# The end of layer 0 written out: the last two rows of a two-layer attention kernel in an order of their own

## The chip, the cores and the metric

The kernel runs on one core of a Trainium2 chip. The metric is the device time of one execution in microseconds (us). Five engines run their own instruction streams and meet at semaphores: TensorE (PE; its weight loads are shown apart as PEld), VectorE (DVE), ScalarE (ACT), GpSimd (POOL) and SyncE (SP), which here issues DMAs.

## The reference

The input x has 128 rows of 256 positions and 256 channels. Two layers follow each other, each of the form "x plus attention of the group-normalised x":

```python
# layer 0: 8 heads of 32 channels; one attention of 256 x 256 in each of the 128 rows
x = x + _L0_conv_ref(_gn(x), pair_repr, gate_proj, qkv_proj, out_proj, bias_proj)
# layer 1: 4 heads of 64 channels, keys at most 16 positions away
x = x + _L1_conv_ref(_gn(x), w_in, b_in, w_out, b_out, 16)
```

In layer 0 a row's attention is

```python
bias = einsum('nijz,zh->nhij', pair_repr, bias_proj)     # the same for all rows
gate = sigmoid(x @ gate_proj)
sim  = softmax(q @ k.T * scale) + bias                   # the bias is added after the softmax
out  = ((sim @ v) * gate) @ out_proj
```

The normalisation `_gn` takes mean and variance over all rows and positions of a group of 8 channels. Layer 1 can therefore not start before the last row of layer 0 has been added up and counted.

## The kernel before

**Layer 0, the steady part.** Rows are numbered s = 0 to 127 (S = 128) and go in pairs. The loop `for s in range(S)` works on row s, finishes row s - 1 and, in the same turn, projects the next pair: q and k in an even turn, values and gate in an odd one (`stretch`). Each projection, each output projection and each bias product of a pair is done with seven block products in place of eight (a Strassen-like scheme: `Seven`, `Output`, `biased`), which needs sums of blocks made beforehand: `sum_values` and `out_sums` on GpSimd, `sum_bias` once on VectorE. One of the four blocks of the bias is overwritten by such a sum; its original is kept in DRAM as `bias_far`, for a fallback that runs only where a softmax sum is out of range.

In a turn, a row passes through these steps:

- `scores(s, half)`, L838 and L851: the products k times q of four heads into four PSUM banks (`sim`), and their exponentials on ScalarE into `ex`, 128x512 each.
- `join_tiles`, L860: VectorE adds the two key tiles of the exponentials (`both`), two heads in one instruction.
- `sum_heads`, L883: TensorE sums `both` over the keys for all eight heads (`zs`).
- `divide`, L963 to L969: VectorE takes the reciprocal `rz`; SP writes it to DRAM (`rz0_far`) and reads it back four times, broadcast over the partitions (`near`). For the last row only, `spread_last` (L981, L982) does this with two TensorE products and a copy.
- `totals` and `least`, L989 and L996: the sum and the minimum of `zs`, for the fallback's condition.
- `attend`, L870: the exponentials times v (`av`, a PSUM bank).
- `biased`, L934 to L956: the bias times v for a pair of rows, seven products in one PSUM bank (`pbv`); after most of them ScalarE or VectorE takes a part out (`bv`).
- `weighted` (L1011) and `gated` (L1023, L1024): av times near, plus bv, times the gate, into `at`.
- `output`, L590 with L701 to L723: the output projection of a pair in seven products (`po`); VectorE takes every one out and adds the row itself (`xt`), into `o`.
- `settle`, L1058: VectorE counts the pair into `stats1` (mean and variance by parts), and SP stores it to DRAM (`x1`).

**Layer 0, the end.** The last turns (s = 126 and 127) are in the same loop with conditions (`s < S - 2`, `s >= S - 2`): no pair is left to project. What remains of the bias products of rows 126-127 and the seven-product output of rows 124-125 runs in them. After the loop, row 127 is finished, and rows 126 and 127 get their output by `one_by_one`: sixteen products, and one addition by VectorE (`finish`, L1050).

**Statistics.** `Most` joins the parts in `stats1` ahead of the end: two shares, one in turn 125 and one in turn 126 (L291 to L295), into a tile `most`. At the end `channel_columns` copies that tile and the three last parts into one tile `last` (L301, L302), joins them (L308), copies the means (L310), and takes the mean and variance over the groups with two small TensorE products (L313, L322). `keep_on` puts products with no use between them (`warm`, L1173).

**Order.** TensorE, ScalarE, VectorE and SP run in the order of the program text in this part (`manual_schedule`); GpSimd's order is the scheduler's. Eight PSUM banks hold all: a ring of five for projections, scores, outputs and `near`, and one each for `zs`, `pbv` and `av`. A product that wants a bank of the ring waits until the one five places earlier has been read out.

**Layer 1** begins with the loads of its first rows (`load1`, L794), VectorE's normalisation (L1237) and the products `p1v` (L1274).

Of the kernel before, what the change touches and what calls it, by code (L numbers as in the profile page):

```python
# [9 lines left out]
F32 = mybir.dt.float32  # L10
# [5 lines left out]
P = 128  # L16
# [23 lines left out]
def conv_preact_kernel(  # L40
# [59 lines left out]
    def strip(a):  # L100
        return slice(B * a, B * (a + 1))
# [173 lines left out]
    class Most:  # L275


        def __init__(self, pool, stats, late, which):
            self.stats, self.late = stats, late
            n = stats.shape[2] - late  # L280
            self.shares = ((0, n // 2), (n // 2, n))
            self.mv = pool.tile([P, 2, 2, 2], F32, name=f"mv_most{which}")

            self.most = pool.tile([P, 2, 2, 3], F32, name=f"most{which}")

        def join(self, share):
            n0, n1 = self.shares[share]
            count = (n1 - n0) * 2.0 * R
            nc.gpsimd.memset(self.most[:, :, share, 0:1], count)
            for half in range(2):  # L290
                nc.vector.bn_aggr(  # L291
                    out=self.mv[:, half, share, :], in_=self.stats[:, half, n0:n1].rearrange("p n s -> p (n s)")
                )
            nc.vector.tensor_copy(self.most[:, :, share, 1:2], self.mv[:, :, share, 0:1])
            nc.vector.tensor_scalar(self.most[:, :, share, 2:3], self.mv[:, :, share, 1:2], count, None, op0=ALU.mult)  # L295

    def channel_columns(pool, most, which, wait=lambda n: None):

        stats, late = most.stats, most.late
        last = pool.tile([P, 2, 2 + 2 * late, 3], F32, name=f"last{which}")  # L300
        nc.vector.tensor_copy(last[:, :, 0:2], most.most)  # L301
        nc.vector.tensor_copy(  # L302
            last[:, :, 2:].rearrange("p h e k -> p h (e k)"),
            stats[:, :, stats.shape[2] - late :].rearrange("p h n s -> p h (n s)"),
        )
        mv = pool.tile([P, 2, 2], F32, name=f"mv{which}")
        for half in range(2):
            nc.vector.bn_aggr(out=mv[:, half, :], in_=last[:, half].rearrange("p e k -> p (e k)"))  # L308
        means = pool.tile([P, 2], F32, name=f"means{which}")
        nc.vector.tensor_copy(means, mv[:, :, 0])  # L310
        wait(5)
# [463 lines left out]
    with ExitStack() as both:  # L775
        st1 = both.enter_context(tc.tile_pool(name="st1", bufs=1))

        stats1 = st1.tile([P, 2, S // 2 + 1, 6], F32, name="stats1")
        quarters1 = {w: Quarters(st1, w_in_t, n * C, f"1{w}") for n, w in enumerate("qk")}
# [17 lines left out]
        with ExitStack() as lay0:  # L797
# [57 lines left out]

            def join_tiles(s, half, j):

                if s < S:
                    ex, both = hd[s, half]
                    nc.vector.tensor_tensor(both[:, j : j + 2], ex[:, j : j + 2, 0, :], ex[:, j : j + 2, 1, :], ALU.add)  # L860

            def products(to, s, weights):

                i, r = divmod(s, 2)
                v = res["v", i]
                for half in range(2):
                    for kt in range(2):
                        for j in range(4):
                            c0 = kt * P + j * D0
                            nc.tensor.matmul(  # L870
                                to[D0 * j : D0 * (j + 1), half, :],
                                lhsT=v[:, 2 * r + half, c0 : c0 + D0], rhs=weights(4 * half + j, kt),
                                start=(kt == 0), stop=(kt == 1),
                            )
# [84 lines left out]
            def divide(s, zs):  # L959
                if s < 0:  # L960
                    return
                rz = att.tile([P, R], F32, tag="rz", name=f"rz{s}", bufs=1)
                nc.vector.reciprocal(rz, zs[:, 0, :])  # L963
                near = att.tile([P, 2, R], F32, tag="near", name=f"near{s}", bufs=1)
                if s < S - 1:
                    far = rz0_far[s % 2]
                    nc.sync.dma_start(out=far.rearrange("j h q -> (j h) q"), in_=rz[0 : P : B // 2])
                    for j in range(A):
                        nc.sync.dma_start(  # L969
                            out=near[strip(j)].rearrange("p h q -> p (h q)"),  # L970
                            in_=far[j].rearrange("h q -> (h q)").partition_broadcast(B),
                        )
                hd[s, "rz"] = rz
                hd[s, "zs"], hd[s, "near"] = zs, near

            def spread_last(s):

                rz, near = hd[s, "rz"], hd[s, "near"]
                ps = proj_bank(f"near{s}")
                for half in range(2):  # L980
                    nc.tensor.matmul(ps[:, half, :], lhsT=spread0[:, half], rhs=rz, start=True, stop=True)  # L981
                nc.scalar.copy(near, ps)  # L982

# [69 lines left out]
            def settle(s, first, k, part):  # L1053
# [3 lines left out]
                for half in range(2):  # L1057
                    nc.vector.bn_stats(out=stats1[:, half, part, :], in_=o[:, first : k + 1, half, :])  # L1058
                if k == XG - 1:
# [20 lines left out]
            with tc.manual_schedule(  # L1080
# [11 lines left out]
                nc.sync.dma_start(out=bias_far, in_=bias_blocks[0, 1])  # L1092
                most1 = Most(st1, stats1, 3, 1)
                for s in range(S):
                    exps = scores(s, 0)
# [20 lines left out]
                    if s % 2 == 0:  # L1116
                        settle_pair((s - 4) // 2)
                    if S - 3 <= s < S - 1:
                        most1.join(s - S + 3)
                    normal(s + 4)  # L1120
                    third, fourth = scores(s, 1)
                    if s % 2 == 1 or s >= S - 2:
                        third()
# [8 lines left out]
                    total = lambda: totals(s - 1)  # L1132
                    rests = iter((third, fourth, total) if s % 2 == 0 and s < S - 2 else (fourth, total))

# [5 lines left out]
                    if s % 2 == 1 and s > 1:  # L1140
                        out_sums((s - 3) // 2)
                        po, work = output((s - 3) // 2, work), ()
                    if s < S - 2:
                        stretch(
                            ("qk", "vg")[s % 2], s // 2 + 1, (EARLY, PLAIN)[s % 2], rest, bias, po,
                            work if s % 2 == 0 else (),
                        )
                        work = work if s % 2 == 1 else ()
                    else:
                        rest()  # L1150
                        for _ in range(2 if s % 2 == 0 else 3):
                            next(bias)
                            next(po, None)
                            next(po, None)
                        for _ in po:
                            pass
                        if s % 2 == 0:
                            next(bias)
                    if s >= S - 2:
                        rest()  # L1160
                    for job in work:
                        job()
                    if s % 2 == 1 and s < S - 2:
                        sum_rows((s + 3) // 2)
                        sum_values(s // 2 + 1)
                load1(0)
                load1(1)
                warm = proj_bank("warm")

# [4 lines left out]

                gated(S - 2)
                outputs.pop(S // 2 - 2).take(4)
                least(S - 2)
                divide(S - 1, sum_heads(S - 1))
                totals(S - 1)
                attend(S - 1)  # L1180
                spread_last(S - 1)
                weighted(S - 1)
                gated(S - 1)
                settle_pair(S // 2 - 2)
                for s in (S - 2, S - 1):
                    if s == S - 1:
                        keep_on(4)
                    for _ in one_by_one(out_sb, st[s]["at"], f"po{s}", lambda ps: st[s].update(po=ps), B):
                        pass
                    finish(s)  # L1190
                mean1, rstd1 = channel_columns(st1, most1, 1, keep_on)
# [379 lines left out]
    with tc.If(sure < P):  # L1571
        with ExitStack() as lay:
# [10 lines left out]
            )  # L1583
            nc.sync.dma_start(out=bias_sb[:, 0, :, P : 2 * P], in_=bias_far)
            stats2 = one.tile([P, 2, S // 2, 6], F32, name="stats2")

# [127 lines left out]
            for g in range(S // XG):  # L1714
                x3 = two.tile([P, XG, 2, R], F32, tag="x3", name=f"x3_{g}")
                nc.sync.dma_start(out=x3, in_=rows(x1, g * XG, XG))
                for k in range(0, XG, 2):
                    for half in range(2):
                        nc.vector.bn_stats(
                            out=stats2[:, half, (g * XG + k) // 2, :], in_=x3[:, k : k + 2, half, :]  # L1720
                        )
            most2 = Most(one, stats2, 1, 2)
            for share in range(2):
# [29 lines left out]
```

## Time and profile before

| | |
|---|---|
| time, median of 3 runs (lowest to highest) | 3100.07 us (3099.98 to 3102.68) |
| the profiled execution: time, span of the core | 3099.65 us, 3098.0 us |
| busy: TensorE, its weight loads | 3009.3 us (97%), 2058.7 us (66%) |
| busy: VectorE, ScalarE, GpSimd | 2259.0 us (73%), 1911.1 us (62%), 1903.9 us (61%) |
| mean granted TensorE clock | 0.992 |
| first score product of row 126 | 1987.67 us |
| first product of layer 1 (p1v) | 2028.60 us |

The span is the time from the first to the last instruction of the core; the execution's time has 1.65 us more. In the lines of the profile "L838" is line 838 of the kernel; a tile's name stands without its number; "out<-in" names what is written and read; "x32" counts instructions as the chip executes them, and one matrix product of 32-bit numbers is two of them. In a timeline the first number is the start in us from the span's start and the second the duration. In the chain of waits a line is a piece of the path that ended last. The granted clock is 1.00 at full speed.

### The profile page before, as it was taken

Reading aid. Unit: us, or ns where it says so; the run is one execution under the profiler, and the core shown is the slowest. Engines: PE = TensorE matmul, PEld = TensorE weight load, DVE = VectorE, ACT = ScalarE, POOL = GpSimd, SP = SyncE. Lnnn points to the kernel's source line nnn. Section 1 sums busy time; section 2 is a strip of 40 time slices with the busy share of each in tenths; the row PEclk is TensorE's granted clock in tenths of the full one; section 3 lists DMA queues with packets and bytes.
Section 4 is the critical chain, followed back from the end, with each engine's and each line's share of the span. In section 5 each row is a group of like instructions: output and inputs, shape, how many; then the busy total and the mean of one; then the engine's idle time right before and its main releaser. Section 6 shows DMA issues by size and latency. Waiting matters only on the chain.

```text
span 3098.0 us, 142607 instructions
## 1 busy us (share of the span) xinstructions
PE 3009.3 (97%) x62733; PEld 2058.7 (66%) x62733; DVE 2259.0 (73%) x4523; ACT 1911.1 (62%) x4321; POOL 1903.9 (61%) x1916
## 2 busy tenths in 40 slices
PE   7779999999999999999999999999999999999997
PEld 4546666666666666666666666567777777777775
DVE  4667787778877887788778877746666666666665
ACT  4656666666666666666666666645555555555553
POOL 3035666666656565656565656457777777767774
PEclk9989999999999999999999999999999999999999
DMA  9942222222222222222222222114444444444443
GB/s 381 424 130 50 56 65 62 57 55 65 61 58 55 65 62 58 55 65 62 60 53 65 62 59 54 58 58 103 98 98 105 98 104 93 103 100 103 99 97 71
DMA packets 384789, 280.86 MB, mean 91 GB/s; under 512 B 285232, under 2 KB 353312, under 8 KB 378016
## 3 DMA queue, kind: packets, MB, share of 16 engines
q1 hardware_dynamic: 383264, 269.29, 32.9%
q8 instruction: 494, 8.09, 1.1%
q0 software_dynamic: 752, 2.36, 0.2%
q14 instruction: 135, 1.11, 0.1%
q10 hardware_dynamic: 144, 0.00, 0.0%
HBM read 202.38 MB, written 69.18 MB: 88 GB/s over the span
## 4 chain that ended last, share of the span: by engine, by line
PE 91%; DMA 5%; DVE 2%; POOL 1%; ACT 0%; issue 0%; SPq 0%; DVEq 0%; POOLq 0%; ACTq 0%
PE sim L838 9%; PE p1v L1274 7%; PE av L870 7%; PE p1q L590 7%; PE pbv L934 6%; PE po L590 6%; PE p1k L590 6%; PE p1o L590 6%; PE pq L590 6%; PE pv L590 6%; PE pk L590 5%; PE pg L590 5%; PE zs L883 4%; PE 1sim L1295 3%; DMA pr<-in_L_conv_pair_repr_dram 3%; PE 1av L1336 3%
## 5 line engine op out<-in xcount | busy, mean ns | idle before, releaser
L851 ACT ACTIVATE ex<-sim 128x512 f32<-128x512 f32 x1024 | 554.8, 605 | 256.6 <-PE sim L838 256.6
L860 DVE TENSOR_TENSOR both<-ex 128x512 f32<-128x512 f32 x512 | 449.5, 897 | 67.0 <-ACT ex L851 66.8
L634 POOL TENSOR_TENSOR v<-v,midv 128x512 f32<-128x512 f32 x64 | 82.1, 1283 | 453.8 <-ACT v L628 453.8
L838 PE MATMUL sim<-q,k 32*64 32x256 f32 x8192 | 289.6, 389 | 1.3 <-ACT ex L851 1.3
L963 DVE RECIPROCAL rz<-zs 128x256 f32<-128x256 f32 x128 | 225.0, 1758 | 67.2 <-PE zs L883 51.9
L870 PE MATMUL av<-ex,v 128*32 128x256 f32 x4096 | 244.5, 379 | 1.6 <-DVE at L1024 1.6
L694 ACT ACTIVATE 1q<-p1q,bqk 128x256 f32<-128x256 f32 x192 | 91.1, 475 | 240.7 <-PE p1q L590 129.7
L1305 POOL TENSOR_TENSOR 1p<-1ex,seen 128x768 f32<-128x768 f32 x127 | 231.6, 1824 | 12.4 <-ACT 1ex L1303 12.4
L1274 PE MATMUL p1v<-w_in_t,1xn 128*64 128x128 f32 x4096 | 236.2, 273 | 0.1
L1274 PEld LDWEIGHTS p1v<-w_in_t,1xn 128*64 128x64 f32 x4096 | 231.4, 137 | 6.1 <-issue 0.5
L838 PEld LDWEIGHTS sim<-q,k 32*64 32x64 f32 x8192 | 152.2, 131 | 113.3 <-issue 66.4
L582 POOL TENSOR_TENSOR 1ts<-1xn 128x512 f32<-128x512 f32 x64 | 81.4, 1272 | 232.0 <-ACT 1xn L1235 232.0
L634 POOL TENSOR_TENSOR q<-q,midq 128x512 f32<-128x512 f32 x64 | 82.0, 1282 | 196.1 <-ACT q L628 196.1
L870 PEld LDWEIGHTS av<-ex,v 128*32 128x32 f32 x4096 | 131.5, 110 | 79.2 <-DVE at L1024 2.1
L1405 DVE TENSOR_TENSOR 1at<-1av,1near 128x512 f32<-128x512 f32 x128 | 82.6, 686 | 132.7 <-DMA 1near<-rz_far 103.6
L1312 POOL TENSOR_TENSOR 1zp<-1p 128x512 f32<-128x512 f32 x127 | 162.4, 1278 | 10.0
L1281 ACT COPY 1v<-p1v 128x512 f32<-128x512 f32 x128 | 75.1, 586 | 125.0 <-PE p1v L1274 125.0
L346 DVE BATCH_NORM_STATS2 stats<-xs 128x6 f32<-128x128 f32 x512 | 100.3, 277 | 63.7 <-DMA xs<-in_x_dram 63.7
L883 PE MATMUL zs<-both,place 128*32 128x256 f32 x2048 | 139.2, 389 | 0.5 <-DVE both L860 0.5
L1023 DVE TENSOR_TENSOR av<-av,bv 128x512 f32<-128x512 f32 x128 | 89.5, 700 | 62.8 <-ACT bv L956 60.5
L1373 DVE RECIPROCAL 1rz<-1z 128x64 f32<-128x64 f32 (+1 forms) x192 | 129.8, 678 | 2.2
L688 DVE SCALAR_TENSOR_TENSOR 1o<-p1o,bo_v,yg 128x256 f32<-128x256 f32 x183 | 88.6, 484 | 56.1 <-PE p1o L590 53.2
(340 smaller groups left out, 8348.9 us busy)
## 6 DMA issues: line engine op xcount, KB each, us to landing
pr<-in_L_conv_pair_repr_dram SPq DMA_DIRECT2D x32, 1024.0 KB
xs<-in_x_dram SPq DMA_DIRECT2D x16, 2048.0 KB
x<-o SPq DMA_DIRECT2D x64, 512.0 KB
yg<-x SPq DMA_DIRECT2D x64, 512.0 KB
out_dram<-1o SPq DMA_DIRECT2D x256, 128.0 KB
near<-rz_far SPq DMA_DIRECT2D x508, 64.0 KB
xg<-in_x_dram SPq DMA_DIRECT2D x252, 128.0 KB
1near<-rz_far SPq DMA_DIRECT2D x124, 256.0 KB
```

Source lines behind the costliest of these rows:

```text
L590: nc.tensor.matmul(out[cols], lhsT=lhsT[:, cols], rhs=rhs, **flags)
L634: nc.gpsimd.tensor_tensor(self.to[:, 2:4], self.to[:, 2:4], self.mid, ALU.add)
L838: nc.tensor.matmul(sims[j][KB * c : KB * (c + 1), kt, :], lhsT=k[p0 : p0 + D0, 2 * r + half, k0 : k0 + KB], rhs=q[p0 : p0 + D0, 2 * r + ha ...
L851: nc.scalar.activation(ex[:, j], sims[j], AF.Exp, scale=1.0 / math.sqrt(D0))
L860: nc.vector.tensor_tensor(both[:, j : j + 2], ex[:, j : j + 2, 0, :], ex[:, j : j + 2, 1, :], ALU.add)
L870: nc.tensor.matmul(to[D0 * j : D0 * (j + 1), half, :], lhsT=v[:, 2 * r + half, c0 : c0 + D0], rhs=weights(4 * half + j, kt), start=(kt == ...
L883: nc.tensor.matmul(zs[strip(j), 0, :], lhsT=place0[:, half, :], rhs=both[:, j, :], start=(half == 0), stop=(half == 1),)
L934: nc.tensor.matmul(ps[strip(j), acc, half, :], lhsT=stationary[n][:, half, strip(j)], rhs=bias_of[n][:, 4 * half + j, :], start=(n <= 2 an ...
L963: nc.vector.reciprocal(rz, zs[:, 0, :])
L1274: nc.tensor.matmul(ps[KB * half : KB * (half + 1), b, :], lhsT=xns[i][:, 2 * r + kt, KB * b : KB * (b + 1)], rhs=w_in_t[:, kt, 2 * C + P * ...
L1305: engine.tensor_tensor(p.rearrange("p j (r c) -> p (j r) c", c=WROW)[:, :, 0 : 2 * WSTEP] .rearrange("p r (t c) -> p r t c", c=WSTEP)[:, : ...
L1312: engine.tensor_tensor(zp, p[:, :, 0:R], p[:, :, R : 2 * R], ALU.add)
```

## The change

The loop ends at row 125, and the rest is written out.

- The first-half scores of a row, its second-half scores and the other row's products are put in one order by hand. Row 126's and 127's scores are issued earlier among the other products.
- The bias products of rows 126 and 127 are plain products by row (`bias_row`: sixteen products by `products`, then one copy) in place of the seven products of the pair. For this the first bias block is read back from `bias_far` into its place after row 125, by SP, ahead of layer 1's first two loads.
- The outputs of rows 124 and 125 are plain too (`plain_output`); ScalarE copies them to a tile `o_last` and GpSimd adds the rows (`residual`).
- The reciprocals of rows 125 and 126 are spread by TensorE (`spread_row`), not through DRAM, as for row 127 before. `keep_av` copies `av` to the SBUF tile, and the product `near` stays in PSUM: the reverse of before.
- GpSimd makes one of the two joins of key tiles (`join_tiles`) of row 126's second half and row 127's first half. For row 127's second half there is none: TensorE sums the exponentials themselves over both key tiles.
- The two joins of statistics come one turn sooner (turns 124 and 125), with four parts left over in place of three. The joined shares stand in `stats1` itself, so the copies L301, L302 and L310 go.
- The same code for statistics serves the fallback, which isn't executed here.

The core of the diff:

```diff
@@ class Most, channel_columns
-            nc.gpsimd.memset(self.most[:, :, share, 0:1], count)
+            most = self.stats[:, :, self.n, 3 * share : 3 * share + 3]
+            nc.gpsimd.memset(most[:, :, 0:1], count)
...
-        last = pool.tile([P, 2, 2 + 2 * late, 3], F32, name=f"last{which}")
-        nc.vector.tensor_copy(last[:, :, 0:2], most.most)
...
         for half in range(2):
-            nc.vector.bn_aggr(out=mv[:, half, :], in_=last[:, half].rearrange("p e k -> p (e k)"))
-        means = pool.tile([P, 2], F32, name=f"means{which}")
-        nc.vector.tensor_copy(means, mv[:, :, 0])
+            nc.vector.bn_aggr(
+                out=mv[:, half, :], in_=most.stats[:, half, most.n :].rearrange("p n s -> p (n s)")
+            )
+        means = mv[:, :, 0]
@@ the spreading of the reciprocals
+            def spread_row(s):
+
+                hd[s, "av"] = ps = proj_bank(f"near{s}")
                 for half in range(2):
-                    nc.tensor.matmul(ps[:, half, :], lhsT=spread0[:, half], rhs=rz, start=True, stop=True)
-                nc.scalar.copy(near, ps)
+                    nc.tensor.matmul(ps[:, half, :], lhsT=spread0[:, half], rhs=hd[s, "rz"], start=True, stop=True)
+
+            def keep_av(s):
+
+                hd[s, "near"] = att.tile([P, 2, R], F32, tag="near", name=f"near{s}", bufs=1)
+                nc.scalar.copy(hd[s, "near"], hd.pop((s, "av")))
@@ the loop
-                for s in range(S):
+                for s in range(S - 2):
...
-                    if S - 3 <= s < S - 1:
-                        most1.join(s - S + 3)
+                    if s >= S - 4:
+                        most1.join(s - S + 4)
@@ after the loop
+                nc.sync.dma_start(out=bias_blocks[0, 1], in_=bias_far)
                 load1(0)
                 load1(1)
...
+            def bias_row(s):
+                to = ps_av.tile([P, 2, R], F32, tag="bv", name=f"pbv{s}")
+                products(to, s, lambda h, kt: bias_sb[:, kt, h, :])
+                return to
+            def plain_output(s):
+                for _ in one_by_one(out_sb, st[s]["at"], f"po{s}", lambda ps: st[s].update(po=ps), B):
+                    pass
+            def residual(s):
+                o = outs[last - 1][:, s % 2]
+                nc.scalar.copy(o, st[s]["po"])
+                nc.gpsimd.tensor_tensor(o, o, st[s]["xt"], ALU.add)
...
+                exps = scores(S - 2, 0)
+                gated(S - 4)
+                outputs.pop(last - 2).take(4)
+                least(S - 4)
+                divide(S - 3, sum_heads(S - 3))
+                run(exps)
+                totals(S - 3)
+                attend(S - 3)
+                keep_av(S - 3)
+                join_tiles(S - 2, 0, 0)
+                join_tiles(S - 2, 0, 2)
+                exps = scores(S - 2, 1)
+                run(exps)
+                spread_row(S - 3)
+                weighted(S - 3)
+                gated(S - 3)
+                plain_output(S - 4)
+                residual(S - 4)
+                join_tiles(S - 2, 1, 0, nc.gpsimd)
+                join_tiles(S - 2, 1, 2)
+                exps = scores(S - 1, 0)
+                run(exps)
+                divide(S - 2, sum_heads(S - 2))
+                totals(S - 2)
+                settle_pair(last - 2)
+                least(S - 3)
+                attend(S - 2)
+                keep_av(S - 2)
+                pbv = bias_row(S - 2)
+                e = res["g", last]
+                nc.scalar.activation(e, e, AF.Tanh, scale=0.5)
+                hd[S - 2] = att.tile([P, 2, R], F32, tag="bv0", name=f"bv{S - 2}", bufs=1)
+                nc.scalar.copy(hd[S - 2], pbv)
+                join_tiles(S - 1, 0, 0, nc.gpsimd)
+                join_tiles(S - 1, 0, 2)
+                exps = scores(S - 1, 1)
+                run(exps)
+                plain_output(S - 3)
+                spread_row(S - 2)
+                weighted(S - 2)
+                gated(S - 2)
+                residual(S - 3)
...
+                least(S - 2)
+                divide(S - 1, zs)
+                totals(S - 1)
+                products(av, S - 1, lambda h, kt: ex1[:, h % 4, kt, :], range(1, 2))
+                keep_av(S - 1)
+                hd[S - 1] = att.tile([P, 2, R], F32, tag="bv1", name=f"bv{S - 1}", bufs=1)
+                nc.scalar.copy(hd[S - 1], bias_row(S - 1))
+                spread_row(S - 1)
+                weighted(S - 1)
+                gated(S - 1)
+                plain_output(S - 2)
+                settle_pair(last - 1)
+                finish(S - 2)
+                plain_output(S - 1)
+                finish(S - 1)
```

## The prediction

> **What bounds the kernel now.** I read the page's chain first: it is TensorE nearly throughout.
>
> ```profile
> PE 91%; DMA 5%; DVE 2%; POOL 1%; ACT 0%; issue 0%; SPq 0%; DVEq 0%; POOLq 0%; ACTq 0%
> ```
>
> So work taken from another engine counts only where TensorE waits. The build orders of both kernels put the change between the first score product of row 126 and the first layer-1 product (p1v): apart from the statistics of rows 124 and 125 and the SP queue, every engine's order outside is the same. In the trace that stretch runs from 1987.67 to 2028.60 us, 40.93 us. The table by stages compares it with the pair of rows ahead of it:
>
> ```profile
> 1959.54:1987.67 28.13, 28.13 (x676) 18.25 (x673) 21.85 (x34) 19.36 (x44) 18.07 (x19) 1.00 0.13 41
> 1987.67:2000.00 12.33, 8.81 (x200) 4.85 (x200) 11.76 (x19) 5.41 (x14) 4.91 (x7) 0.91 0.21 67
> ```
>
> First busy column: PE; third: DVE; the third from the end: granted clock. Rows 124-125 are TensorE alone; in row 126 TensorE stands for 3.5 us and VectorE is 95% busy. There is no next pair to project, so nothing fills TensorE while it waits. A finer table shows a second loss:
>
> ```profile
> 1993.00:1997.00 4.00, 0.79 (x24) 0.38 (x16) 3.96 (x9) 2.01 (x5) 0.00 (x0) 1.00 0.30 92
> 1998.00:2001.00 3.00, 3.00 (x44) 1.35 (x48) 2.35 (x4) 1.80 (x6) 0.44 (x1) 0.50 0.09 29
> ```
>
> After four microseconds with 0.79 us of products the granted clock is 0.50 for three. The chain of waits, in order of time, shows all of this:
>
> ```profile
> 1996.83 0.34 DVE bv L946
> 1997.17 0.14 issue
> 1997.30 0.64 PE pbv L934 x16
> 1997.95 1.94 PE sim L838 x32
> 1999.89 1.67 PE zs L883 x16
> 2001.56 0.44 PE pbv L934 x16
> 2001.99 1.73 PE av L870 x32
> 2003.72 1.05 PE sim L838 x32
> ...
> 2010.75 0.44 DVE o L707
> 2011.18 0.04 issue
> 2011.23 0.68 PE po L590 x8
> ```
>
> The third bias product waits for VectorE (it is behind the row sums, statistics and their join), then scores and head sums take 1.94 and 1.67 us at half clock, against 1.05 for the scores at 2003.72. From 2005.34 the seven-product output of rows 124-125 and VectorE take turns on one PSUM tile: seven rounds, 2005.16 to 2012.51, with a product of 0.43 and a wait each. The end is VectorE's (timeline):
>
> ```profile
> 2019.39 0.69 DVE L1024 SCALAR_TENSOR_TENSOR at<-g,av 128x512 f32<-128x512 f32 x1
> 2020.00 1.28 DVE L1058 BATCH_NORM_STATS2 stats<-o 128x6 f32<-128x512 f32 x2
> 2021.36 0.69 DVE L1050 TENSOR_TENSOR o<-po,xt 128x512 f32<-128x512 f32 x1
> 2022.09 0.75 DVE L1058 BATCH_NORM_STATS2 stats<-o 128x6 f32<-128x256 f32 x2
> 2022.99 0.69 DVE L1050 TENSOR_TENSOR o<-po,xt 128x512 f32<-128x512 f32 x1
> ```
>
> **The change, part by part.** I lay the new order out along TensorE with start-to-start times of this trace.
>
> *Scores early.* Four half-row scores stay, 4 x 1.05 = 4.20. They now run between other products, so their exponentials (2.06 us for four tiles) lie beside TensorE work.
>
> *Plain bias for rows 126-127.* Removed: seven products of 0.44 = 3.1 us and their VectorE and ScalarE steps. Added: two row products of the attention product's form (32 recorded matmuls of 128x256): 1.73 each, 3.46. On TensorE it costs 0.4 us; what goes is the alternation. It needs the first bias block back, so SP gets a 512 KB reload, which waits for product 7 of rows 124-125 (1982.7). Layer 1's first two loads stand behind it, earlier than now (issued 2007.02). The trace has 1 MB of such loads issued at 2007.02 and the traffic over by 2012; even three times that would end before the first plain bias product, some 12 us into the stretch (about 1999.4). Priced at nothing; uncovered it would cost what it is late.
>
> *Plain outputs for rows 124-125.* Removed: the seven rounds, 7.35 us of path. Added: two outputs like those of rows 126-127 (2017.20 to 2019.06: 1.86 at most; 1.73 by the attention product's row), 3.6 together. Copy and residual go to ScalarE (0.59) and GpSimd (1.28); nobody waits for these until the statistics 10 us later.
>
> *Quotients by product (rows 125, 126).* Ten DMAs leave SP; two products of the L981 kind come, start to start 1.06 (2016.14 to 2017.20). With row 127's, 3 x 1.06 = 3.18. ScalarE copies the attention tile to SBUF (0.6 each).
>
> *Head sums, attention products.* Head sums start to start 0.90 (1988.72 to 1989.61) for eight products: 1.8 for rows 125-126. Row 127 sums its second half straight from the exponentials: twelve products, 1.35. Three attention products: 5.19.
>
> TensorE work up to row 126's output: 4.20 + 3.46 + 3.6 + 3.18 + 1.8 + 1.35 + 5.19 = 22.8 us.
>
> *Waits that come.* (a) Row 124's output wants the PSUM bank of the first exponential of row 126's second half, which is on ScalarE behind the totals and the copy of row 125: 0.2 to 0.6. (b) The fourth score bank of row 127 is row 125's quotient bank, free when VectorE has gated it: 0.4. (c) Row 126's quotient product wants an exponential of row 127, on ScalarE behind totals (0.37), copy (0.49), tanh (0.95) and bias copy (0.49); the totals wait for VectorE's minimum, behind the reciprocal (1.67) and the statistics of rows 122-123 (1.2): 0.5 to 0.8. Together 1.1 to 1.8; I take 1.3. Longest TensorE wait: under 1 us, so by the stage above (0.79 us of work in 4) the clock stays at 1.00.
>
> *The tail.* After row 127's quotient product VectorE is the path: multiply, add, gate 3 x 0.73 = 2.2 (2017.92 to 2020.00 is 2.1); statistics of rows 124-125 1.2 to 1.36; two outputs with statistics, 2 x (0.73 + 0.67), unbroken now since row 127's output is ready before VectorE is; then aggregate to p1v, 3.88 (2024.72 to 2028.60), less the means copy (0.18), and the two copies ahead of it (0.34) are gone too. 2.15 + 1.3 + 2.8 + 3.7 = 9.95, say 10.0.
>
> Sum: 22.8 + 1.3 + 10.0 = 34.1 against 40.9: 6.8 us less. The same bookkeeping laid over the old order, with its half-clock stage, gives 40.6 for the measured 40.9, so single steps are good to some tenths.
>
> *Joins of statistics sooner.* A join (1.82 + 0.25 on VectorE) moves from row 125 to 124 and one from 126 to 125. Behind it in row 124 wait a tile sum and the bias add; VectorE idles there 2.10 us before 1969.87, so it fits. Without that cover: 2 us.
>
> *Tile sums on GpSimd.* Half the sums of two half rows go to GpSimd. VectorE's and GpSimd's adds hold each other up in this trace:
>
> ```profile
> 1935.28 2.25 DVE L860 TENSOR_TENSOR both<-ex 128x512 f32<-128x512 f32 x2
> ```
>
> Two sums take 2.25 us beside GpSimd adds, one alone 0.68; that is 0.45 each. In the new order GpSimd's sum of a half row starts at its second exponential, VectorE's a microsecond later: about half a us apart for row 126, clear for row 127. I price it at 0; 0.9 if both meet, none if not. The Trainium skill ("SBUF — State Buffer", section "Who interferes with whom") speaks against this part more strongly: a VectorE instruction with two SBUF inputs and a reading GpSimd instruction exclude each other for a whole instruction. By that rule each meeting could cost a GpSimd add of 1.28 us, and the sum would lose up to 2.6 us.
>
> The profiled execution has 3099.65 us (span 3098.0); the median of the three is 3100.07, 0.42 above. 3100.07 - 6.8 = 3093.3; layer 1 keeps its order, so all of it shows at the end.
>
> **The rivals.**
>
> *The single-file queues take half back.* ScalarE and VectorE now carry the row in an order where one late step holds three engines; if each of the waits (a), (b), (c) is a microsecond longer, and one tile sum meets GpSimd, about 3.2 us go: 3096.4. For it: (c) hangs on five steps in a row. Against: ScalarE is busy for 44% of row 126's stage and VectorE loses some 10 steps.
>
> *The clock drops once more.* If a wait grows enough that four microseconds hold under 1 us of products, the 0.50 stage comes back: 3 us at half speed, 1.6 us lost: 3094.8. Against: some product is due every microsecond.
>
> *Slower: the clock stays low.* With the rows no longer fed by a steady alternation, TensorE at 0.50 would stretch its 22.8 us of path work to twice that. The change is lost when 6.8 us of this work run at half clock, some 14 us of time; at 20 us of time (10 us of work) the kernel takes 3103.3. Only a profile with long low-clock stages between 1988 and 2015 would show it; the nearest row is 3 us long, so it is unlikely.
>
> *It doesn't act.* If VectorE, not TensorE's alternation, sets rows 126-127, little would move. VectorE has 32.9 us busy in the 40.9; the change takes about 7 us of it away (bias and output steps, two tile sums, copies), so this is a part of the first rival.
>
> **How the numbers follow.** The forecast, 5.4 to 8.4 us gained: 0.64. Queues (2.5 to 5): 0.22. One clock drop (4.5 to 6): 0.10. Slower: 0.04. The bound of 0.2% (6.2 us, 3093.9; about what a measurement of this kernel can tell from no change) cuts through the forecast: spread evenly over 5.4 to 8.4, 0.47 would lie beyond; I put 0.55 there, since the centre is 6.8 and (a) to (c) add up to 1.1 at their lower ends. So faster 0.55, within 0.41 (the rest of the forecast, the queues, the clock), slower 0.04. The range for 8 in 10 reaches from a gain of 9.2 (no waits 1.3, a tail shorter by 0.3, and 0.8 of bookkeeping error) to one of 3.3 (queues): 3090.9 to 3096.8.
>
> **What would show it.** Right: p1v starts 34 us after row 126's first score; no stage below clock 1.00 in it; the chain is TensorE up to row 126's output with three waits under 1 us, then VectorE; the seven rounds gone; the reload landed long before the plain bias product. Wrong: a TensorE wait above 1 us at the quotient products, tile sums of over 1 us on VectorE, a stage at 0.50, row 125 longer than 15.8 us (1971.86 to 1987.67) because of the join, or a layer 1 longer than the 1069.4 us from p1v to the span's end.

## The result and the profile after

The changed kernel takes 3092.16 us (median of 9 runs, 3089.78 to 3093.6) against 3100.33 us before (9 runs beside them, 3098.98 to 3102.68): a ratio of 0.9971, 95% interval 0.9963 to 0.998. 3093.3 was predicted.

The profiled execution has 3092.16 us with a span of 3090.2. Row 126's first score product starts at 1986.08 and p1v at 2020.01 us: a stretch of 33.93 us where it was 40.93. 34.1 was predicted.

The share of the chain of waits by engine is nearly as it was (DMA has 4% where it had 5%), since the stretch is 1% of the span:

```profile
PE 91%; DMA 4%; DVE 2%; POOL 1%; ACT 0%; issue 0%; SPq 0%; DVEq 0%; POOLq 0%; ACTq 0%
```

The table by stages of the kernel after (columns as before: time, PE, PEld, DVE, ACT, POOL, granted clock, DMA) shows the pair of rows 124-125, the 12.33 us that answer to the stage shown of before, and then the stretch in its two parts, up to row 126's output and from there to p1v:

```profile
1957.95:1986.08 28.13, 28.13 (x677) 18.29 (x673) 23.77 (x38) 19.36 (x44) 17.57 (x19) 1.00 0.23 71
1986.08:1998.41 12.33, 12.33 (x240) 6.92 (x240) 9.34 (x13) 7.83 (x17) 5.69 (x6) 1.00 0.32 105
1986.08:2009.92 23.84, 23.84 (x425) 13.78 (x421) 15.44 (x21) 14.13 (x32) 6.98 (x7) 1.00 0.24 78
2009.92:2020.01 10.09, 9.26 (x89) 6.10 (x89) 8.23 (x22) 1.51 (x2) 0.52 (x3) 1.00 0.17 57
```

The first line is 28.13 us as before, to the hundredth: VectorE has 1.9 us more to do there (the earlier join) and it costs nothing. In the second TensorE is busy throughout (8.81 before) and VectorE 9.34 (11.76). The clock is 1.00 everywhere. The chain, in order of time, is now TensorE alone up to row 126's output:

```profile
1990.97 1.06 PE near L979 x4
1992.04 1.86 PE po L587 x32
1993.90 1.65 PE sim L836 x32
1995.55 1.00 PE zs L881 x16
1996.55 1.73 PE av L868 x32
1998.27 1.73 PE pbv L868 x32
2000.00 1.05 PE sim L836 x32
2001.05 1.86 PE po L587 x32
2002.91 1.09 PE near L979 x4
```

The steps are the quotient product, row 124's output, row 127's scores, head sums, attention, the plain bias product, scores, row 125's output and the second quotient product. One step is longer than its work: the scores at 1993.90, 1.65 against 1.05. The end is VectorE's, unbroken from the gate on (timeline):

```profile
2011.63 0.69 DVE L1026 SCALAR_TENSOR_TENSOR at<-g,near 128x512 f32<-128x512 f32 x1
2012.24 1.28 DVE L1060 BATCH_NORM_STATS2 stats<-o_last 128x6 f32<-128x512 f32 x2
2012.46 1.93 PE L587 MATMUL po<-at,out_sb 128*32 128x256 f32 x32 [0.61 <-DVE at L1026]
2013.43 0.68 DVE L1052 TENSOR_TENSOR o<-po,xt 128x512 f32<-128x512 f32 x1
2014.14 0.75 DVE L1060 BATCH_NORM_STATS2 stats<-o 128x6 f32<-128x256 f32 x2
2014.81 0.67 DVE L1052 TENSOR_TENSOR o<-po,xt 128x512 f32<-128x512 f32 x1
2015.52 0.75 DVE L1060 BATCH_NORM_STATS2 stats<-o 128x6 f32<-128x256 f32 x2
```

SP issues the reload of the bias block 16 us before the plain bias product (1998.09) and layer 1's loads right behind it; the traffic that follows is over by 1992 (224 GB/s from 1990 to 1991, 4 from 1991 to 1992), six microseconds ahead of that product:

```profile
1981.88 0.60 SPq L1156 DMA_DIRECT2D bias_sb<-bias_far  x1
1982.53 1.28 SPq L792 DMA_DIRECT2D yg<-x  x2
```

### The profile page after: what moved, and what is told of

Read it like the earlier page. It is cut to its first block, busy times and chain, and to the rows that moved or that the text cites. A ratio compares the mean times of both kernels' runs of the same rounds, so it can differ in the third digit from the quotient of the medians.

```text
span 3090.2 us, 142498 instructions
## 1 busy us (share of the span) xinstructions
PE 3004.1 (97%) x62701; PEld 2061.0 (67%) x62701; DVE 2251.8 (73%) x4506; ACT 1911.6 (62%) x4323; POOL 1903.1 (62%) x1913
## 3 DMA queue, kind: packets, MB, share of 16 engines
q0 software_dynamic: 752, 2.36, 0.2%
## 4 chain that ended last, share of the span: by engine, by line
PE 91%; DMA 4%; DVE 2%; POOL 1%; ACT 0%; issue 0%; SPq 0%; DVEq 0%; POOLq 0%; ACTq 0%
PE sim L836 9%; PE av L868 7%; PE p1v L1346 7%; PE p1q L587 7%; PE po L587 6%; PE pbv L932 6%; PE p1k L587 6%; PE p1o L587 6%; PE pv L587 6%; PE pq L587 6%; PE pk L587 5%; PE pg L587 5%; PE zs L881 4%; DMA pr<-in_L_conv_pair_repr_dram 4%; PE 1sim L1367 3%; PE 1av L1408 3%
```

## The experiments

The measure in all of them is the stretch from row 126's first score product to p1v, read from one profile each; the ratio to the kernel before (with its 95% interval) stands beside it.

| kernel | stretch, us | ratio to before |
|---|---|---|
| before; before again | 40.93; 40.92 | again: 1.0002 [0.9993, 1.0011] |
| after; after again | 33.93; 33.94 | 0.9971 [0.9963, 0.998]; 0.9968 [0.9957, 0.9979] |
| after, outputs of rows 124-125 in seven products | 39.11 | 1.0002 [0.9993, 1.0011] |
| after, bias of rows 126-127 in seven products | 37.14 | 0.9987 [0.9978, 0.9996] |
| after, quotients of rows 125-126 through DRAM | 37.64 | 0.9985 [0.9976, 0.9994] |
| after, all tile sums on VectorE | 34.64 | 0.9967 [0.9955, 0.9979] |
| before, statistics part alone | 38.33 | 0.9987 [0.9978, 0.9996] |
| before, plain outputs of rows 124-125 alone | 38.57 | 0.9987 [0.9978, 0.9996] |
| before, both of these | 37.37 | 0.9986 [0.9977, 0.9995] |
| after, two statistics steps moved | 33.66 | 0.997 [0.9959, 0.9981] |
| after, these moved and row 127's end in halves | 33.43 | 0.9974 [0.9965, 0.9983] |

**The seven-product output, put back into the new order.**

```diff
-                plain_output(S - 4)
-                residual(S - 4)
+                out_sums(last - 1)
...
-                plain_output(S - 3)
+                run_out = output(last - 1, ())
+                for _ in run_out:
+                    pass
+                outputs.pop(last - 1).take(4)
...
-                residual(S - 3)
```

> The new order with the seven-product output of rows 124-125 put back, in one piece where the plain output of row 125 stands. The stretch (first score product of row 126 to first p1v) was 40.93 us before and is 33.93 in the changed kernel. Theory (the gain is mostly TensorE no longer taking turns with VectorE on one PSUM tile): seven rounds of about 1.05 us replace two plain outputs of 1.9 less the GpSimd work, so the stretch is 37.5 to 38.5 and about 4 of the 7 us are lost; the clock stays at 1.00. Rival (the order of the scores and the missing low-clock stage carry the gain, and the form of the output does not matter): the stretch stays at 34 to 35.

39.11 us: 5.2 us of the 7.0 are gone, rather more than expected. The timeline shows the alternation, seven products of 0.64 us with a wait of 0.5 to 0.6 us between them, 1.2 to 1.3 us from start to start:

```profile
2001.86 0.64 PE L587 MATMUL po<-at,out_sb 128*32 128x256 f32 x8
2003.04 0.64 PE L587 MATMUL po<-at,out_sb 128*32 128x256 f32 x8 [0.55 <-DVE o L720]
2004.32 0.64 PE L587 MATMUL po<-att,sums_o 128*32 128x256 f32 x8 [0.64 <-DVE o L698]
```

From 2001.86 to the quotient product at 2009.80 they take 7.94 us; the two plain outputs took 1.87 and 1.89. That is 4.2 of the 5.2. Another 0.9 comes ahead of it, most of it at row 127's first scores (2.26 us start to start against 1.64): with row 124's output gone, nothing covers row 125's gating.

**The seven-product bias, put back.** Its products are spread between the others; the block isn't read back.

```diff
+                bias = biased(last)
+                next(bias)
...
-                pbv = bias_row(S - 2)
+                next(bias)
...
-                hd[S - 1] = att.tile([P, 2, R], F32, tag="bv1", name=f"bv{S - 1}", bufs=1)
-                nc.scalar.copy(hd[S - 1], bias_row(S - 1))
```

> The new order with the seven-product bias of rows 126-127 put back, its products spread between the other products; the first bias block is not read back (only the fallback, which does not run, would need it). TensorE's own work falls by 0.4 us, but after most products ScalarE or VectorE has to empty the one PSUM bank. Theory (the waits for that bank are what the plain products remove): the stretch is 35.5 to 37 against 33.93, with TensorE waits of 1 to 2 us before bias products. Rival (the old place of the bias products, behind the statistics, was the trouble, and the form costs nothing): 33.5 to 34.5.

37.14 us, 3.2 more, a little over the theory's range. TensorE's waits of the stretch now include (total, times, longest):

```profile
PE pbv L932 <- ACT bv L948: 1.4, 1, 1.4
PE near L979 <- DVE rz L961: 1.3, 1, 1.3
PE pbv L932 <- DVE bv L952: 0.5, 1, 0.5
```

They add up to 3.2 us: a bias product waits for the copy that empties its only bank, behind whatever ScalarE or VectorE does first; and row 127's quotient product waits for the reciprocal, which the second plain bias product had covered.

**The quotients through DRAM, put back.**

```diff
-                if s >= S - 3:
+                if s >= S - 1:
                     return
...
-                keep_av(S - 3)
...
-                spread_row(S - 3)
```

> The new order with the quotients of rows 125 and 126 sent through DRAM again, and the attention tile left in PSUM. Theory (the quotient products cost TensorE 1.06 us each and the transfer of about 6 us lies beside other work): one TensorE wait of about 3 us appears at the head sums of row 126, the two products of 1.06 us and the wait for their bank go, and the stretch is 33.2 to 34.5, the same within half a microsecond. Rival (the transfer is what held row 126 before): 36 or more.

The theory failed; 37.64 is the rival's range. The timeline shows why:

```profile
1992.92 0.59 SPq L967 DMA_DIRECT2D rz_far<-rz  x1
1994.69 2.59 SPq L969 DMA_DIRECT2D near<-rz_far  x4
1999.12 0.70 DVE L1013 TENSOR_TENSOR av<-av,near 128x512 f32<-128x512 f32 x1 [5.08 <-DMA near<-rz_far]
2001.19 0.68 DVE L858 TENSOR_TENSOR both<-ex 128x512 f32<-128x512 f32 x1
2001.93 0.56 PE L881 MATMUL zs<-both,place 128*32 128x256 f32 x2 [3.93 <-DVE both L858]
```

From SP's first issue to VectorE's use it takes 6.2 us. VectorE works in order, so a tile sum of row 126 that needs no quotient stands behind that wait, and TensorE behind the sum: 3.93 us. TensorE stands almost still from 1998 to 2002, and the 3.4 us that follow run at half clock as well (a stage of each; granted clock third from the end):

```profile
1998.00:2002.00 4.00, 0.07 (x4) 0.07 (x8) 2.69 (x4) 1.10 (x3) 1.26 (x1) 1.00 0.04 16
2003.00:2004.00 1.00, 1.00 (x14) 0.45 (x10) 1.00 (x1) 0.00 (x0) 0.00 (x0) 0.50 0.00 0
```

**All tile sums on VectorE.**

```diff
-                join_tiles(S - 2, 1, 0, nc.gpsimd)
+                join_tiles(S - 2, 1, 0)
...
-                join_tiles(S - 1, 0, 0, nc.gpsimd)
+                join_tiles(S - 1, 0, 0)
```

> The changed kernel with the two tile sums of row 126's second half and row 127's first half that GpSimd makes given back to VectorE. Theory (as priced: GpSimd's sums are worth nothing, TensorE is the path here and the sum on VectorE, 0.68 us each, ends before the head sums ask for it): the stretch stays at 33.7 to 34.2 us. Rival (VectorE's queue is the tight one, so each sum of 0.68 us delays the head sums of rows 126 and 127, and what is behind them): 34.6 to 35.4 us. Third (the port shared by VectorE and GpSimd cost something after all): below 33.6 us.

34.64 us: the rival's lower end, 0.7 more than after. The timeline names one place:

```profile
1996.65 2.36 DVE L858 TENSOR_TENSOR both<-ex 128x512 f32<-128x512 f32 x2
1997.07 1.40 POOL L1178 TENSOR_TENSOR o_last<-o_last,xt 128x512 f32<-128x512 f32 x1 [6.81 <-ACT o_last L1177]
1999.31 0.39 PE L881 MATMUL zs<-both,place 128*32 128x256 f32 x2
```

Two sums beside GpSimd's addition of row 124 take 2.36 us, where two alone take 1.22 (1992.49 in the same trace). The last head sums wait for the second, and the reciprocal of row 126 starts 0.7 us later than after (11.23 against 10.53 us into the stretch). Row 127's sums, with no addition beside them, take 1.28 and cost nothing. So GpSimd's share is worth 0.7 us, because of that one meeting.

**The statistics part alone, in the old order.** Two copies and the copy of the means go, the joins come a turn sooner.

```diff
-                    if S - 3 <= s < S - 1:
-                        most1.join(s - S + 3)
+                    if S - 4 <= s < S - 2:
+                        most1.join(s - S + 4)
```

> The kernel before with the statistics part alone: joins in turns 124 and 125, four late parts, no copies of the joined parts. Its first join of row 126's turn (2.1 us on VectorE) stood on the chain ahead of the third bias product. Theory (it frees that product, but the seven rounds and the other bias waits remain, and four of the copies at the end go): the stretch is 38 to 39.5 against 40.93, about 2 of the 7 us, and the clock stage at 0.50 is shorter or gone. Rival (nothing else is early, so it only moves the wait): 40.3 to 41.

38.33 us, 2.6 less than before. Row 127's second-half scores come 13.79 us into the stretch instead of 15.98. Of these 2.2 us, 0.9 is the third bias product's wait (0.71 us, 1.59 before: the join no longer stands ahead of it) and 1.3 the half clock, which is absent. The remaining 0.4 us is at the end, where the copies went.

**The plain outputs alone, in the old order.**

```diff
-                    if s % 2 == 1 and s > 1:
+                    if s == S - 1:
+                        po = plain_pair(S - 4)
+                    elif s % 2 == 1 and s > 1:
```

> The kernel before with one part of the change alone: the outputs of rows 124 and 125 as two plain products of 1.86 us, copied by ScalarE and added by GpSimd, in place of the seven products that take turns with VectorE. Theory (the alternation with VectorE is what costs, 5.2 us of the 7.35 in the new order; in the old order the stage at half clock ahead of it stays): 38.3 to 39.3 us from row 126's first score to p1v, against 40.9, with the stage at clock 0.50 still there. Rival (the outputs take turns with other waits of this row anyhow, so the plain ones only wait elsewhere): 40.4 us or more. Third (the full gain of the seven rounds shows at once): 36.5 us or less.

38.57 us, as the theory had it; over 3 us still run at clock 0.50. In the new order the same part is worth 5.2.

**Both of these**, the two edits in one kernel.

> The kernel before with two parts of the change: the statistics part (38.33 us alone) and the plain outputs of rows 124-125 (38.57 alone). Theory (the parts stand at different places of the stretch, so their gains of 2.6 and 2.4 add up, and the low-clock stage is gone as with the statistics part alone): 35.6 to 36.4 us. Rival (they save the same idle time of VectorE): 37.5 us or more. If it is 36, the two parts with the seven-product bias and the quotients through DRAM left as they were have 5 of the 7 us.

37.37 us, between theory and rival. The half clock is back, though TensorE's work and waits ahead of it are those of the statistics part alone: 1.93 us before the second bias product and 0.71 before the third. Four microseconds of each kernel that start at the same point of the row, and a stage behind them, in the table by stages; first both parts:

```profile
1994.00:1998.00 4.00, 1.37 (x44) 0.88 (x48) 2.97 (x7) 1.92 (x5) 0.00 (x0) 1.00 0.33 100
1999.00:2001.00 2.00, 2.00 (x32) 0.79 (x20) 1.39 (x2) 1.41 (x3) 0.00 (x0) 0.50 0.09 28
```

then the statistics part alone:

```profile
1992.75:1996.75 4.00, 1.37 (x44) 0.88 (x46) 2.96 (x7) 1.93 (x5) 0.00 (x0) 1.00 0.36 101
1997.75:1999.75 2.00, 1.95 (x48) 1.17 (x48) 1.93 (x3) 1.92 (x4) 0.40 (x1) 1.00 0.08 26
```

Both have 1.37 us of products in 4; behind one the clock is 0.50, behind the other 1.00.

The traces show what differs. The granted clock changes on a grid of 3.41 us: the low stage lasts 3.41 us in each of the five traces that have one in the stretch (with both parts 1998.32 to 2001.74), and in the trace of before the last change ahead of the one at 1997.81 is at 229.71, 518 times 3.4133 us earlier. The grid lies elsewhere against the stretch in every execution. The step of the grid ahead of the low stage, and that stage, with both parts:

```profile
1994.91:1998.32 3.41, 1.64 (x48) 1.17 (x56) 2.38 (x6) 1.30 (x5) 0.00 (x0) 1.00 0.47 146
1998.32:2001.74 3.42, 3.42 (x60) 1.63 (x44) 2.29 (x5) 2.61 (x8) 0.00 (x0) 0.50 0.25 85
```

The same two steps with the statistics part alone, where the grid is counted on from its last change (229.35 us):

```profile
1994.04:1997.45 3.41, 2.01 (x64) 1.37 (x64) 2.37 (x5) 1.30 (x5) 0.00 (x0) 1.00 0.60 184
1997.45:2000.87 3.42, 3.37 (x80) 1.83 (x64) 3.35 (x5) 3.12 (x7) 1.44 (x2) 1.00 0.16 50
```

The steps begin 6.33 and 6.71 us into the stretch. The later one takes in more of row 127's first-half scores, 2.01 us of products where the other has 1.64. In the five traces with a low stage the step ahead of it holds 0.12 (quotients through DRAM), 0.64 (plain outputs alone), 1.01 and 1.15 (before again, before) and 1.64 us; no other step in the stretches of the thirteen traces holds less than 1.75 us, and the clock stays at 1.00 behind all of them. This is read from the traces and not tested: no run moves the grid alone. Outside the stretch steps with 1.4 to 2.5 us went either way, so the busy time of a step isn't the whole rule.

The low stage with both parts costs 1.4 us up to row 127's second-half scores (15.16 us into the stretch against 13.79). Without it both parts together would stand at about 36.0, the sum of the two gains; that last step is worked out, not measured.

**The two kernels once more**, without an edit.

> The changed kernel once more, without an edit, as the measure for other runs and to see how the last rows and the rest of the program repeat. Theory (the gain lies in the last rows alone): 33.9 us again, plus or minus 0.2, from row 126's first score to p1v; ratio to the kernel before 0.9976 to 0.9980 (7.0 us of 3101 is 0.9977); what the medians of the first comparison showed beyond 7.0 us is spread of the rest of the program. Rival (the rest of the program got faster too, by about 1.2 us): ratio 0.9972 or lower again, and layer 1 from p1v to the span's end shorter than the 1069.4 us before.

> The kernel before once more, without an edit. The whole time has fallen by 8 to 9 us at the medians where the stretch from row 126's first score to p1v fell by 7.0 in the two profiles. Theory (the rest is spread of loads at the start and of layer 1, which the edit doesn't touch): the stretch is 40.9 us again, plus or minus 0.3, and the time before and after it differs from the first profile by up to 2 us either way. Rival (the stretch of the kernel before is itself longer in other executions, since its low-clock stage varies): 41.5 us or more, or a low-clock stage longer than 3.2 us.

The stretches repeat to 0.01 us. Before again has its stage at 0.50 in the same place. The whole time doesn't follow the stretch as closely: the medians fall by 8.2 and 9.3 us in the two comparisons, the stretch by 7.0. By after again's own measures (ratio 0.9968, layer 1 at 1068.5 us) the rival would be right. The profiles of all kernels together speak against it: up to row 126's first score it is 1987.71 us on average in the five profiles with the old order and 1987.74 in the eight with the new one; from p1v to the span's end 1069.38 and 1069.36. Single profiles lie within 1985.7 to 1988.8 and 1068.1 to 1071.3. So the profiles show a gain in the stretch alone. A fall of 7.0 us would be a ratio of 0.9977, which lies inside both intervals, so the medians' further 1 to 2 us can be spread; where they come from isn't settled.

**Two statistics steps moved.** Rows 122-123 are counted after the minimum that ScalarE waits for, rows 124-125 ahead of row 127's last multiplication.

```diff
-                settle_pair(last - 2)
                 least(S - 3)
...
                 join_tiles(S - 1, 0, 2)
+                settle_pair(last - 2)
...
                 spread_row(S - 1)
+                settle_pair(last - 1)
                 weighted(S - 1)
...
-                settle_pair(last - 1)
                 finish(S - 2)
```

> The changed kernel with two statistics steps of VectorE moved: that of rows 122-123 (1.22 us) from ahead of the minimum of row 125's sums to behind the join of row 127's first half, and that of rows 124-125 (1.28 us) from the tail, where VectorE is the path, to ahead of row 127's last multiplication, where VectorE waits 1.76 us for TensorE's quotient product. Theory (the tail of 10.1 us is VectorE's work laid end to end, so what fills VectorE's idle time ahead of it leaves it; the step runs into the multiplication's start by some tenths): the stretch falls by 0.5 to 1.1 us, to 32.8 to 33.4. Rival (the rows of 124-125 are not ready by then, or VectorE's step ends later than the quotient product by as much as it saves): 33.8 to 34.3 us.

33.66 us, between the two: 0.3 less than after, where the theory had 0.5 to 1.1. Row 126's output starts at the same point as after (23.81 us into the stretch; 23.84), so the earlier minimum bought nothing. In the tail 1.28 us left VectorE's queue, but now VectorE waits for TensorE:

```profile
2014.30 1.93 PE L587 MATMUL po<-at,out_sb 128*32 128x256 f32 x32 [0.61 <-DVE at L1026]
2016.30 0.69 DVE L1052 TENSOR_TENSOR o<-po,xt 128x512 f32<-128x512 f32 x1 [0.74 <-PE po L587]
```

The tail of after has two paths: VectorE's queue, and row 127's gate with the output product behind it. In after VectorE adds row 127's output 2.35 us after that product starts, here 2.00: the second path was only 0.35 us shorter, and it takes over.

**And row 127's end in halves.**

```diff
+                for kt in range(2):
+                    nc.vector.scalar_tensor_tensor(
+                        at[:, kt], res["g", last][:, 2 + kt, :], 1.0, t[:, kt], op0=ALU.add, op1=ALU.mult
+                    )
...
+                for m in range(2):
+                    nc.vector.tensor_tensor(o[:, m], ps[:, m], xt[:, m], ALU.add)
+                    nc.vector.bn_stats(out=stats1[:, m, most1.entry(last + 1), :], in_=o[:, m, :])
```

> The changed kernel with the two statistics steps moved as before (33.66 us) and row 127's last steps in halves: VectorE gates half of the channels, TensorE begins the output's products with it, and VectorE adds and counts the first half of the output while TensorE makes the second. Theory (with the statistics out of the way the end is gate, 1.93 us of products, addition and statistics one after the other, and halves overlap them): 33.0 to 33.4 us. Rival (two steps of half size cost VectorE as much more as they save): 33.6 us or more.

33.43 us, at the edge of the theory. TensorE's wait for the gate falls from 0.61 to 0.35 us and VectorE's for the output from 0.74 to 0.42:

```profile
2014.85 1.93 PE L587 MATMUL po<-at,out_sb 128*32 128x256 f32 x32 [0.35 <-DVE at L1255]
2016.84 0.42 DVE L1269 TENSOR_TENSOR o<-po,xt 128x256 f32<-128x256 f32 x1 [0.42 <-PE po L587]
```

It has the shortest stretch of all, 0.5 us below after. The whole time (3092.68 us, 11 runs) can't show that: its ratio's interval overlaps that of after.

## Why the prediction was right

**The sum.** Predicted were 24.1 us up to row 126's output and 10.0 for the tail; measured 23.84 and 10.09. The gain of the stretch was put at 6.8 and is 7.0. The predicted time is 1.1 us too high, mostly because the medians fell by 1.2 us more than the stretch, which lies within the interval of the ratio.

**TensorE's work: 22.8 predicted, 23.25 measured.** Scores (4.20), head sums (3.1) and quotient products (3.18) came out as taken from before. The wide products were mis-sized by about 0.1 each: bias 3.72 against 3.46, the first two outputs 3.76 against 3.6, attention 5.29 against 5.19. The 1.73 us in the sum was the chain's piece, which begins when the step ahead of it has drained; start to start the same product took 1.83 (2001.82 to 2003.65 before).

**The waits: 1.3 predicted, 0.6 measured.** (a) isn't there: from the quotient product to row 124's output it is 1.06 us, like the other two. (b) is: the scores of row 127 take 1.64 us start to start instead of 1.05, and after six weight loads of theirs TensorE loads none from about 1994.0 to 1994.4, while VectorE's gate (1993.61 + 0.69) ends; 0.6 against 0.4. (c) isn't: row 125's output to the second quotient product is 1.89 us, row 124's to its successor 1.87. ScalarE did get its minimum late (it waited 2.3 us for it), but the copies behind were done in time. The run with the minimum earlier agrees: row 126's output came no sooner. So the work was 0.45 too low and the waits 0.7 too high, and the sum was good because the two nearly cancelled.

**The priced-at-nothing edits.** The earlier joins and the reload cost nothing, as put (28.13 us for rows 124-125 in both kernels). The tile sums on GpSimd were priced at zero, which holds for after: they meet no VectorE sum. That they gain 0.7 us was not in the prediction, since the sum assumed VectorE would make its own in time. Where a meeting does happen it costs 1.1 us (2.36 against 1.22 in the run with VectorE's sums), more than the 0.9 taken for two: the prediction set the 2.25 us of two sums against twice the 0.68 of a single one, but two alone take 1.22. The Trainium skill ("SBUF — State Buffer", "Who interferes with whom") has the two engines lock each other out for an instruction; a GpSimd addition takes 1.28 us, and the measured 1.1 lies near that rule.

**The clock.** It stayed at 1.00, as predicted, but the rule behind it was too loose. "Four microseconds with 0.79 us of products" was taken as the stage that lowers it, and the rival asked for under 1 us in four. With both parts in the old order a step of the 3.41 us grid that held 1.64 us was enough. The steps of after hold 2.80 us or more, so it kept clear of that; the nearest of the new order that stayed at 1.00 is the seven-product output, with a step of 1.75. The Trainium skill ("TensorE: Matmul & The Clock Gate", Part 1) says that activity is watched in a free-running window of about 3.4 us, of which it speaks for the rise to full clock, and that the low clock comes after at least one idle window. The grid of 3.41 us agrees with the first; a step with 1.64 us of products, where no TensorE wait was longer than 1.93 us, is not idle and lowered the clock all the same. One low-clock stage costs 1.3 to 1.4 us here; the rival put 1.6.

**The rivals.** The single-file queues exist: through DRAM, one late landing held VectorE, then TensorE for 3.93 us, and then the clock. Plain quotient products are what keeps that from happening, a gain which the prediction never priced, since it saw only the ten DMAs leave. "It doesn't act" is out: the outputs, the bias and the quotients, undone one at a time, cost 5.2, 3.2 and 3.7 us. Nothing of "the clock stays low" was seen. No run undoes the hand-made order of the scores, so its own share of the 7.0 us isn't measured. (The rival's own terms, three waits of a microsecond and one tile sum of 0.45, add up to about 3.45, not 3.2.)

**Layer 1** took 1070.2 us, longer than the 1069.4 that the prediction named as a sign of error; repeats lie between 1068.1 and 1071.3, so that sign couldn't tell anything.

## What to carry to other kernels

At the end of a pipeline, where no other work fills TensorE, a scheme with fewer products but an engine's step between each two loses to plain products: seven products took 7.94 us, two plain outputs of more work 3.76. Parts of such a rewrite are not additive: undone one at a time they cost 5.2, 3.2 and 3.7 us of a total of 7.0, and one that gains 5.2 in the new order gains 2.4 in the old one. The runs above show one reason: a plain product also covers another step's wait (row 125's gating, row 127's reciprocal). Lay the new order out along its bottleneck engine start to start, and price waits one by one: that gave the total of the stretch within 0.2 us, but partly by luck, since the work was 0.45 too low and the waits 0.7 too high.

## What the runs showed of the hardware

- The granted clock fell to 0.50 for 3.41 us in the stretch of five of the thirteen traces, each time behind a step of 3.41 us with 0.12 to 1.64 us of products. The steps lie on a grid that each execution places elsewhere: with the same gaps (1.93 and 0.71 us) the clock fell in one run and stayed at 1.00 in another, whose step held 2.01 us.
- A quotient's way through DRAM and back, broadcast over the partitions, took 6.2 us from SP's first issue to the first use; 2.59 us of it were the four issues of the reads.
- Two VectorE additions of 128x512 in SBUF take 1.22 us alone and 2.36 beside one GpSimd addition, which itself goes from 1.28 to 1.40. In after the same GpSimd addition starts (1994.63) during a VectorE sum that began at 1994.21: the sum keeps its 0.68 us and the addition takes 1.41.
